# A Mamba block with an MLP and experts on one core: the order of products in the MLP's second bank, regrouped weights, four projections in another bank, and a later pin for the statistics

## Chip, core and metric

The kernel runs as one program on one core of a Trainium2 chip, in fp32. The metric is the device time of one execution in microseconds (us); lower is better. The engines are named as in the profile: PE is TensorE's matrix multiplication and PEld its loading of weights, DVE is VectorE, ACT is ScalarE, POOL is GpSimd, SP is SyncE, which here only starts DMAs. A line such as L422 is a line of the kernel before.

## What is computed

The input x has 2048 tokens (T) of 512 channels (D). Cut to what matters here:

```
u   = layernorm(x)
h   = u + mamba2(rmsnorm(u))            # in_proj 512->2576, causal conv of 4, scan in chunks of 128,
                                        # gated rmsnorm, out_proj 1024->512
x   = x + h + (silu(h2 @ gate) * (h2 @ up)) @ down       # h2 = rmsnorm(h), 512->2048->512
out = x + experts(layernorm(x))         # top 2 of 8 experts
```

## The kernel before

**Mamba.** The tokens are worked through in 8 blocks b of 256, each of two chunks of 128; t is the chunk, 0 to 15. While the chunks of block b are computed, `prepare(b + 1)` and `project(b + 1, ...)` make the next block's input.

`prepare` computes the layernorm statistics of its two chunks in `scales`: bn_stats and bn_aggr (L145, L146, VectorE), a square root (L190, ScalarE), a reciprocal (L191, VectorE). It normalizes to hn (L215, VectorE) and transposes hn on TensorE (L197); VectorE writes the transposed tile out of its bank with the norm weight (L201). The input projection is L333, its copy out of the bank L345 (ScalarE), the convolution L352 and L354 (VectorE) with L360 (ScalarE), and small halo copies L346, L347 (POOL).

`chunk` does one chunk's scan in pieces. POOL masks cum (L307). Two products are scaled by exponentials (L414, ScalarE, and L416, VectorE), VectorE makes xd (L422), and TensorE accumulates py (L432, L440) in bank y of pool `ps_y`, and the new state pst (L447) in bank tr. VectorE adds the skip term (yd, L453), adds to the state (L463) and multiplies by the gate (zs, L456). ScalarE squares zs (L476, L477), POOL sums the squares (L479), and TensorE adds over partitions (pms, L489, bank tr). L380 transposes the next chunk's x (ptx, bank tr). The projection po (L486) goes into bank y again. VectorE reads po at L497 to form h; POOL adds h to x (L498), ScalarE's queue stores that (L499), ScalarE squares h (L502), VectorE scales it (L505), and TensorE transposes h for the MLP (L197, bank tr; out by L201).

**MLP.** It works on 4 blocks fb of 512 tokens and 16 groups c of 128 hidden columns. The 512x512 tokens and channels, and the weights, are cut in halves and combined, so that one column group takes seven products of two matmuls each, 128x256, instead of eight. Four go to bank x1 (px) and three to bank x2 (py); each bank has one buffer while the MLP runs between Mamba pieces and two in the last block. In program order the px products are called first, t2, t3 and t4 here, the py products 2, 5 and 3:

- step 1: px first (copied by ScalarE, L760), then one py product, then a down projection pd (L699, added to the rows by VectorE, L700);
- step 2: px t2 (copied by ScalarE, L767), then one py product;
- step 3: px t3 (added to up by VectorE, L774), then one py product;
- step 4: px t4 (multiplied into a by VectorE, L779; POOL multiplies the other half, L780), then the other down projection.

Product 2 is added to a's first half by VectorE (L742) and goes through silu on ScalarE (L743). Product 5 is copied to up by ScalarE (L754). Product 3 adds onto product 5's result in the bank; VectorE adds it to a's second half (L748), and silu follows (L749). Product 3 so comes behind product 5 in any order, and it may write only when the copy L754 has read. Before, group 0 of each block takes 2, 5, 3, the others 5, 3, 2:

```
order = [p2, p5, p3] if c == 0 else [p5, p3, p2]
```

The weights of a group come in two tiles, early and late. In the first MLP block POOL forms sums and differences from the loaded weights (L530, L531, L541, L542) and stores both tiles to DRAM (L543, L544), from where the later blocks load them (L533, L546). The sums L530 and L531 of every group are pinned behind the squares' sums of chunk 1 (`summed_first`), which matters for the first groups.

**Order of the work.** A planner orders each engine's instructions by its own estimates. `tc.high_priority(AT_ONCE)` puts an instruction ahead of others; `tc.issue_after(x)` keeps instructions behind x on the same engine. TensorE alone follows the program's order from block 2 on. MLP blocks 0, 1 and 2 run between the Mamba pieces of blocks 2 to 7, two Mamba blocks for one MLP block, and the experts' routing between those; MLP block 3 runs alone from about 1080 us, and the experts come last. In `chunk`, `behind` and `newest_xd` remember the xd instructions (L422); `prepare` pins blocks 1 and 2 behind `behind`.

Of the kernel before, what the change touches and what calls it, by code (L numbers as in the profile page):

```python
# [8 lines left out]
F32 = mybir.dt.float32  # L9
I32 = mybir.dt.int32  # L10
AF = mybir.ActivationFunctionType
ALU = mybir.AluOpType
# [3 lines left out]
P = 128  # L16
T = 2048
D = 512
NK = D // P
# [5 lines left out]
NCH = TB // P  # L25
# [3 lines left out]
BPF = FB // TB  # L29
DFF = 2048  # L30
FH = FB // 2
FC = 128
NFC = DFF // FC
# [17 lines left out]
def mamba_mlp_moe(ctx, tc, x, w_in, w_out, w_gu, w_down, par, wr, wg, wu, wd, out):  # L51
# [3 lines left out]
    nc = tc.nc  # L55
# [9 lines left out]
    scratch = ctx.enter_context(tc.tile_pool(name="scratch", bufs=1, space=bass.MemoryType.DRAM))  # L65
# [26 lines left out]
    def load_w_in(pair):  # L92
# [15 lines left out]
        out=tri, in_=ones, pattern=[[1, P]], compare_op=ALU.is_ge, fill=0.0, base=0, channel_multiplier=-1  # L108
    )
    late = pw.tile([P, P], F32, name="late")  # L110
    nc.gpsimd.affine_select(
        out=late, in_=ones, pattern=[[-1, P]], compare_op=ALU.is_gt, fill=0.0, base=0, channel_multiplier=1
# [16 lines left out]
        out=upto, in_=ones[:, : NE * NE].rearrange("p (e f) -> p e f", e=NE), pattern=[[1, NE], [-1, NE]],  # L129
# [20 lines left out]
    early = const.tile([P, 1], F32, name="early")  # L150
# [18 lines left out]
    ps_y = psa_stack.enter_context(tc.tile_pool(name="ps_y", bufs=1, space=PSUM))  # L169
# [3 lines left out]
    def bank(kind, shape, name):  # L173
        pool, tag = use[kind]
        return pool.tile([P, *shape], F32, name=name, tag=tag)
# [10 lines left out]
    def scales(b):  # L186
        lo, hi = b * NCH, (b + 1) * NCH
        for t in range(lo, hi):
            stats(wa, res[t], mv[:, t, :])
        nc.scalar.activation(rboth[:, lo:hi], mv[:, lo:hi, 1], AF.Sqrt, bias=eps2, scale=1.0 + EPS)  # L190
        nc.vector.reciprocal(rboth[:, lo:hi], rboth[:, lo:hi])  # L191
# [11 lines left out]
    behind = None  # L203

    def prepare(b):
# [1 line left out]
        nonlocal behind  # L207
        hT = wa.tile([P, NK, TB], F32, name=f"hT{b}", tag="hT")
        hns = []
        with tc.issue_after(behind) if b in (1, 2) else ExitStack():  # L210
            scales(b)
            for j in range(NCH):
                t = b * NCH + j
                hns.append(wa.tile([P, D], F32, name=f"hn{t}", tag="tok", bufs=3))
                nc.vector.tensor_scalar(  # L215
                    hns[j], res[t], mv[:, t, 0:1], rboth[:, t : t + 1], ALU.subtract, ALU.mult
                )
        for j in range(NCH):
# [3 lines left out]
            if b == 0:  # L222
                behind = turned
# [19 lines left out]
        v, u, s, s2, acc = (small(n, 1) for n in ("v", "u", "s", "s2", "acc"))  # L243
# [142 lines left out]
    newest_xd = summed_first = None  # L386
    summed = None

    def chunk(b, j, dt, ncum, dtdec, cd, cum, ec, xb, cs, zs):

        nonlocal summed, summed_first, behind, newest_xd
        t = b * NCH + j
# [4 lines left out]
        y = zs[:, :, tok]  # L397

        for gp in range(2):
# [19 lines left out]
            if gp == 0 and t < NT - 1:  # L419
# [6 lines left out]
                behind, newest_xd = newest_xd or behind, added.ins  # L426
# [48 lines left out]
        with tc.high_priority(AT_ONCE):  # L475
            nc.scalar.activation(sq[:, 0:4, :], y[:, 0:4, :], AF.Square)  # L476
            nc.scalar.activation(sq[:, 4:8, :], y[:, 4:8, :], AF.Square)  # L477
            for n in (4, 2, 1):
                summed = nc.gpsimd.tensor_tensor(sq[:, 0:n, :], sq[:, 0:n, :], sq[:, n : 2 * n, :], ALU.add).ins  # L479
        if t == 1:  # L480
            summed_first = summed
        yield

        po = ps_y.tile([P, D], F32, name=f"po{t}", tag="y")
        for m in range(8):
            nc.tensor.matmul(po, y[:, m, :], w_o[:, m, :], start=(m == 0), stop=(m == 7))  # L486
        yield
# [28 lines left out]


    KH = NK // 2
    early_d = [scratch.tile([P, 3, KH, FC], F32, name=f"early{c}", tag=f"early{c}") for c in range(NFC)]
    late_d = [scratch.tile([P, 4, KH, FC], F32, name=f"late{c}", tag=f"late{c}") for c in range(NFC)]  # L520

    def load_early(fb, c):

        w = pmlp.tile([P, 4, KH, FC], F32, name="mg", tag="mg", bufs=3)
        if fb == 0:
            nc.sync.dma_start(out=w[:, 0], in_=w_gu[c, :, 0, 0])
            nc.sync.dma_start(out=w[:, 1], in_=w_gu[c, :, 1, 1])
            nc.sync.dma_start(out=w[:, 3], in_=w_gu[c, :, 1, 0])
            with tc.issue_after(summed_first):
                nc.gpsimd.tensor_tensor(w[:, 1], w[:, 3], w[:, 1], ALU.add)  # L530
                nc.gpsimd.tensor_tensor(w[:, 2], w[:, 1], w[:, 0], ALU.subtract)  # L531
        else:
            nc.sync.dma_start(out=w[:, 0:3], in_=early_d[c])  # L533
        return w

    def load_late(fb, c, w):

        v = pmlp.tile([P, 4, KH, FC], F32, name="ms", tag="mg", bufs=3)
        if fb == 0:
            nc.sync.dma_start(out=v[:, 2:4], in_=w_gu[c, :, :, 1])  # L540
            nc.gpsimd.tensor_tensor(v[:, 0], w[:, 0], w[:, 3], ALU.subtract)  # L541
            nc.gpsimd.tensor_tensor(v[:, 1], v[:, 2], w[:, 2], ALU.subtract)  # L542
            nc.gpsimd.dma_start(out=early_d[c], in_=w[:, 0:3])  # L543
            nc.gpsimd.dma_start(out=late_d[c], in_=v)  # L544
        else:
            nc.sync.dma_start(out=v, in_=late_d[c])  # L546
        return v

    def load_down(c):
# [152 lines left out]
    def feed_forward(fb):  # L702

        nonlocal mlp_w, newest
        if fb == 0:
            w = load_early(0, 0)
            mlp_w = w, load_late(0, 0, w)
        b11, b21, b22, t1, t2, t3, t4 = sums(fb)
        rows = []
        pair = None  # L710
        made = {}

        def product(ps, w, m, first=True):
            for k in range(KH):
                nc.tensor.matmul(  # L715
                    ps, w[:, k], m[:, k], start=(first and k == 0), stop=(k == KH - 1), skip_group_check=True
                )

        early, late = mlp_w
        for c in range(NFC):
            more = fb < NFB - 1 or c < NFC - 1
            to = (fb, c + 1) if c < NFC - 1 else (fb + 1, 0)
            if more:
                coming = load_early(*to)
            if c == 1:
                for j in range(NJ):
                    rows.append(wk.tile([P, D], F32, name=f"r{fb}_{j}", tag="row", bufs=5))  # L730
                    nc.sync.dma_start(out=rows[j], in_=resd[fb * NJ + j])
            if c > 1 and c % 2 == 0:
                pair = [made.pop(n) for n in (c - 2, c - 1)]
            a = wk.tile([P, 2, FH], F32, name=f"a{fb}_{c}", tag="a", bufs=4)
            up = wk.tile([P, FH], F32, name=f"up{fb}_{c}", tag="up", bufs=2)
            x1 = bank("g", [FH], f"px{fb}_{c}")
            x2 = bank("u", [FH], f"py{fb}_{c}")

            def p2():
                product(x2, late[:, 2], b21)  # L740
                with tc.high_priority(AT_ONCE):
                    nc.vector.tensor_tensor(a[:, 0], a[:, 0], x2, ALU.add)  # L742
                nc.scalar.activation(a[:, 0], a[:, 0], AF.Silu)  # L743

            def p3():
                product(x2, late[:, 1], b22, False)
                with tc.high_priority(AT_ONCE):
                    nc.vector.tensor_tensor(a[:, 1], a[:, 1], x2, ALU.add)  # L748
                nc.scalar.activation(a[:, 1], a[:, 1], AF.Silu)  # L749

            def p5():
                product(x2, early[:, 1], t1)
                with tc.high_priority(AT_ONCE):
                    nc.scalar.copy(up, x2)  # L754


            order = [p2, p5, p3] if c == 0 else [p5, p3, p2]
            product(x1, early[:, 0], b11)
            with tc.high_priority(AT_ONCE):
                nc.scalar.copy(a[:, 0], x1)  # L760
            order[0]()
            if pair:
                mlp_down(fb, rows, 2 * (c % 2), pair)
            yield
            product(x1, early[:, 2], t2, False)
            with tc.high_priority(AT_ONCE):
                nc.scalar.copy(a[:, 1], x1)  # L767
            order[1]()
            if more:
                coming = coming, load_late(*to, coming)  # L770
            yield
            product(x1, late[:, 0], t3, False)
            with tc.high_priority(AT_ONCE):
                nc.vector.tensor_tensor(up, up, x1, ALU.add)  # L774
            order[2]()
            yield
            product(x1, late[:, 3], t4, False)
            with tc.high_priority(AT_ONCE):
                nc.vector.tensor_tensor(a[:, 0], a[:, 0], x1, ALU.mult)  # L779
            nc.gpsimd.tensor_tensor(a[:, 1], a[:, 1], up, ALU.mult)  # L780
            if pair:
                mlp_down(fb, rows, 2 * (c % 2) + 1, pair)
            newest = a.rearrange("p h q -> p (h q)")
            made[c] = newest, load_down(c)
            if more:
                early, late = coming
            yield
        if more:
            mlp_w = coming
        pair = [made.pop(n) for n in (NFC - 2, NFC - 1)]  # L790
        for j in range(NJ):
            mlp_down(fb, rows, j, pair)
        yield
        yield from route(fb, rows)

    coming = prepare(0)
    for _ in range(3):
        hT = next(coming)  # L800
# [393 lines left out]
```

## Time and profile before

| | |
|---|---|
| three runs | 1588.06, 1590.36, 1590.94 us |
| median | 1590.36 us |
| profiled execution: its own time | 1588.24 us |
| its span | 1586.2 us |
| mean granted clock of TensorE | 0.991 |

The profile is of one execution. Its span runs from its first to its last instruction; 2.0 us of its time lie around that. Busy time counts an engine's own instructions. A timeline's row has start, duration, engine, line, operation, output <- inputs, shapes and count; brackets at its end give the idle time of the engine just before and what ended it, where that is known ("issue" is a wait for nothing that the profile shows). A row with several instructions prints the time from the first's start to the last's end. A list of waits has the total idle time, the times and the longest. Windows give each engine's busy time in a stretch, the instructions in brackets, and the granted clock, where 1.00 is full speed.

### The profile page before, as it was taken

What the parts mean: (1) busy time and instruction counts of PE and PEld (TensorE: products, weight loads), DVE (VectorE), ACT (ScalarE), POOL (GpSimd) and SP (SyncE); (2) the same over time, 40 slices, a digit from 0 to 9 for tenths busy, and PEclk for the clock granted to TensorE, in tenths of its full rate; (3) what the DMA queues carried; (4) which work ended last, traced back from release to release, by engine and by line L of the source; (5) the groups of instructions that cost most, each with busy time, mean ns of one, the idle gap of its engine ahead of it and who ended that gap; (6) DMA issues with size and microseconds to landing.
All of it is one profiled execution on the core that took longest, in us unless ns stands there. A gap on an engine that the chain in (4) does not pass through costs nothing. (4 is left out here: it accounts for less than half of the span.)

```text
span 1586.2 us, 19139 instructions
## 1 busy us (share of the span) xinstructions
PE 1543.2 (97%) x6308; PEld 1052.1 (66%) x6308; DVE 776.1 (49%) x2018; ACT 726.8 (46%) x1325; POOL 427.1 (27%) x542
## 2 busy tenths in 40 slices
PE   9999999999999999999999999999999999999996
PEld 7556576667676776766676667666777666655553
DVE  7586765645647365546555454434454352222221
ACT  6786866836683775456546533222211221111110
POOL 3543335434342212121212212011111123333331
PEclk9899999999999999999999999999999999999999
DMA  9444434644544454343354432229777233333332
GB/s 313 123 127 155 131 124 165 207 145 155 163 166 166 159 181 129 112 135 120 107 171 143 166 107 87 90 90 298 241 239 237 83 61 61 66 63 64 67 67 34
DMA packets 126432, 218.68 MB, mean 138 GB/s; under 512 B 11584, under 2 KB 71488, under 8 KB 126336
## 3 DMA queue, kind: packets, MB, share of 16 engines
q1 hardware_dynamic: 105088, 166.08, 33.1%
q0 software_dynamic: 12320, 35.13, 9.8%
q10 hardware_dynamic: 8928, 16.26, 2.8%
q8 instruction: 52, 0.85, 0.2%
q14 instruction: 44, 0.36, 0.1%
HBM read 176.01 MB, written 41.42 MB: 137 GB/s over the span
## 5 line engine op out<-in xcount | busy, mean ns | idle before, releaser
L699 PE MATMUL pd<-md,a 128*128 128x512 f32 x512 | 239.2, 594 | 0.0
L333 PE MATMUL pm<-hT,wi 128*128 128x256 f32 x768 | 182.7, 384 | 0.8 <-ACT pre L345 0.8
L700 DVE TENSOR_TENSOR r<-r,pd 128x512 f32<-128x512 f32 x128 | 87.4, 684 | 148.6 <-PE pd L699 147.8
L333 PEld LDWEIGHTS pm<-hT,wi 128*128 128x128 f32 x768 | 141.0, 190 | 25.1 <-issue 6.1
L699 PEld LDWEIGHTS pd<-md,a 128*128 128x128 f32 x512 | 97.5, 191 | 75.2 <-issue 66.6
L354 DVE SCALAR_TENSOR_TENSOR ca<-pre,params,ca 128x256 f32<-128x256 f32 x288 | 140.4, 541 | 0.3
L780 POOL TENSOR_TENSOR a<-a,up 128x256 f32<-128x256 f32 x64 | 47.9, 748 | 315.9 <-DVE up L774 256.7
L715 PE MATMUL py<-h2T,ms 128*128 128x256 f32 x512 | 132.0, 380 | 0.9 <-ACT up L754 0.7
L333 PE MATMUL pz<-hT,wi 128*128 128x256 f32 x512 | 122.5, 393 | 1.1 <-DMA wi<-in_w_in 1.1
L1050 PE MATMUL epg<-ew,xgT 128*128 x312 | 118.1, 460 | 0.4 <-issue 0.2
L1050 PE MATMUL epu<-ew,xgT 128*128 x312 | 117.8, 459 | 0.0
L486 PE MATMUL po<-w_o,zs 128*128 128x512 f32 x256 | 113.3, 593 | 1.1 <-DVE yd L453 0.8
L333 PEld LDWEIGHTS pz<-hT,wi 128*128 128x128 f32 x512 | 98.5, 198 | 18.2 <-issue 3.7
L1071 PE MATMUL epd<-ew,ehT 128*128 (+1 forms) x234 | 107.1, 593 | 1.0 <-DVE ehT L1064 1.0
L715 PEld LDWEIGHTS py<-h2T,ms 128*128 128x128 f32 x512 | 95.0, 190 | 17.7 <-DVE a L748 1.9
L414 ACT ACT_TABLE_LOAD x66 | 84.7, 1283 | 34.6 <-DVE ncum L281 33.0
L414 ACT ACTIVATE cum<-cum,ncum 128x128 f32<-128x128 f32 x256 | 85.6, 393 | 13.3 <-POOL cum L307 11.7
L486 PEld LDWEIGHTS po<-w_o,zs 128*128 128x128 f32 x256 | 48.1, 190 | 57.5 <-issue 53.3
L1031 POOL DMA_INDIRECT xg<-xnd,idx x39 | 38.7, 991 | 175.6 <-PE pt L197 173.6
L1050 PEld LDWEIGHTS epu<-ew,xgT 128*128 128x128 f32 x312 | 59.3, 190 | 33.0
L1077 POOL DMA_INDIRECT out<-ey,idx x39 | 62.0, 1590 | 67.0 <-DVE ey L1076 40.8
L199 ACT COPY xgT<-pt 128x512 f32<-128x512 f32 x39 | 22.8, 586 | 117.7 <-PE pt L197 117.7
(250 smaller groups left out, 2577.9 us busy)
## 6 DMA issues: line engine op xcount, KB each, us to landing
wi<-in_w_in SPq DMA_DIRECT2D x80, 512.0 KB, 3.8
ms<-late SPq DMA_DIRECT2D x48, 512.0 KB, 3.8
mg<-early SPq DMA_DIRECT2D x48, 384.0 KB, 3.1
md<-in_w_down SPq DMA_DIRECT2D x64, 256.0 KB, 3.9
cum<-rowsd SPq DMA_DIRECT2D x32, 512.0 KB, 4.5
late<-ms POOLq DMA_DIRECT2D x16, 512.0 KB, 4.3
ec<-rowsd SPq DMA_DIRECT2D x60, 128.0 KB, 4.0
xnd<-xn ACTq DMA_DIRECT2D x28, 256.0 KB, 4.0
```

Of the source, the lines that this page charges most:

```text
L333: nc.tensor.matmul(pm[:, m, :], w[:, k, m * P : (m + 1) * P], hT[:, k, :], start=(k == 0), stop=(k == NK - 1))
L354: nc.vector.scalar_tensor_tensor(ca, pre[:, m, k : k + TB], cw[:, k : k + 1], ca, ALU.mult, ALU.add)
L414: nc.scalar.activation(lt[:, half, i], lt[:, half, i], AF.Exp, bias=ncum[:, j, h : h + 1])
L486: nc.tensor.matmul(po, y[:, m, :], w_o[:, m, :], start=(m == 0), stop=(m == 7))
L699: nc.tensor.matmul(pd, a[:, j * P : (j + 1) * P], d, start=(m == 0), stop=(m == 1))
L700: nc.vector.tensor_tensor(rows[j], rows[j], pd, ALU.add)
L715: nc.tensor.matmul(ps, w[:, k], m[:, k], start=(first and k == 0), stop=(k == KH - 1), skip_group_check=True)
L780: nc.gpsimd.tensor_tensor(a[:, 1], a[:, 1], up, ALU.mult)
L1031: nc.gpsimd.indirect_dma_start(out=xg, out_offset=None, in_=src, in_offset=bass.IndirectOffsetOnAxis(ap=idx[:, n : n + 1], axis=0))
L1050: nc.tensor.matmul(ps, xT[:, k, :], w[:, lo : lo + EI], start=(k == 0), stop=(k == NK - 1))
L1071: nc.tensor.matmul(pd, hT[:n, m, :], w[:n, NG + m * D : NG + (m + 1) * D], start=(m == 0), stop=(m == len(ET) - 1))
L1077: nc.gpsimd.indirect_dma_start(out=out, out_offset=bass.IndirectOffsetOnAxis(ap=idx[:, n : n + 1], axis=0), in_=y, in_offset=None, compute ...
```

## The change

In the second bank all groups take products 2, 5, 3. So the weights for product 2 are needed in step 1, for product 5 in step 2 and for product 3 in step 3, and the tiles are regrouped: early has four parts, late three. The host lays out the gate and up weights so that a group's four parts, gate top, gate bottom, up top, up bottom, are contiguous and arrive in the first MLP block by one DMA of 512 KB where there were three of 128 KB; what late loads is one part instead of two. In later blocks early is 512 KB instead of 384 and late 384 instead of 512.

The pin of the POOL sums on the weights is the squares' sums of chunk 0 instead of chunk 1. In the order of instructions on POOL six operations on the weights of groups 0 and 1, with three DMA issues, then stand between chunk 0's squares' sums and chunk 0's residual add L498; one mask of chunk 2 (L307) stands between the second and the third issue.

The projections po of chunks 0 to 3 are written to bank x1, which the MLP does not use until chunk 4. The statistics and hn of blocks 3 to 7, not pinned before, stand behind the newest xd.

```
-        with tc.issue_after(behind) if b in (1, 2) else ExitStack():
+        with tc.issue_after(behind if b < 3 else newest_xd) if b else ExitStack():
...
-        if t == 1:
+        if t == 0:
             summed_first = summed
...
-        po = ps_y.tile([P, D], F32, name=f"po{t}", tag="y")
+        po = ps_y.tile([P, D], F32, name=f"po{t}", tag="y") if t >= BPF * NCH else bank("g", [D], f"po{t}")
...
-    early_d = [scratch.tile([P, 3, KH, FC], F32, name=f"early{c}", tag=f"early{c}") for c in range(NFC)]
-    late_d = [scratch.tile([P, 4, KH, FC], F32, name=f"late{c}", tag=f"late{c}") for c in range(NFC)]
+    early_d = [scratch.tile([P, 4, KH, FC], F32, name=f"early{c}", tag=f"early{c}") for c in range(NFC)]
+    late_d = [scratch.tile([P, 3, KH, FC], F32, name=f"late{c}", tag=f"late{c}") for c in range(NFC)]
...
         if fb == 0:
-            nc.sync.dma_start(out=w[:, 0], in_=w_gu[c, :, 0, 0])
-            nc.sync.dma_start(out=w[:, 1], in_=w_gu[c, :, 1, 1])
-            nc.sync.dma_start(out=w[:, 3], in_=w_gu[c, :, 1, 0])
+            nc.sync.dma_start(out=w, in_=w_gu[c])
             with tc.issue_after(summed_first):
-                nc.gpsimd.tensor_tensor(w[:, 1], w[:, 3], w[:, 1], ALU.add)
-                nc.gpsimd.tensor_tensor(w[:, 2], w[:, 1], w[:, 0], ALU.subtract)
+                nc.gpsimd.tensor_tensor(w[:, 3], w[:, 2], w[:, 3], ALU.add)
+                nc.gpsimd.tensor_tensor(w[:, 2], w[:, 3], w[:, 0], ALU.subtract)
         else:
-            nc.sync.dma_start(out=w[:, 0:3], in_=early_d[c])
+            nc.sync.dma_start(out=w, in_=early_d[c])
...
-            nc.sync.dma_start(out=v[:, 2:4], in_=w_gu[c, :, :, 1])
-            nc.gpsimd.tensor_tensor(v[:, 0], w[:, 0], w[:, 3], ALU.subtract)
-            nc.gpsimd.tensor_tensor(v[:, 1], v[:, 2], w[:, 2], ALU.subtract)
-            nc.gpsimd.dma_start(out=early_d[c], in_=w[:, 0:3])
-            nc.gpsimd.dma_start(out=late_d[c], in_=v)
+            nc.sync.dma_start(out=v[:, 2], in_=w_gu[c, :, 3])
+            nc.gpsimd.tensor_tensor(v[:, 0], v[:, 2], w[:, 2], ALU.subtract)
+            nc.gpsimd.tensor_tensor(v[:, 1], w[:, 1], w[:, 2], ALU.subtract)
+            nc.gpsimd.dma_start(out=early_d[c], in_=w)
+            nc.gpsimd.dma_start(out=late_d[c], in_=v[:, 0:3])
...
-                product(x2, late[:, 2], b21)
+                product(x2, early[:, 1], b21)
...
-                product(x2, early[:, 1], t1)
+                product(x2, early[:, 3], t1)
...
-            order = [p2, p5, p3] if c == 0 else [p5, p3, p2]
...
-            order[0]()
+            p2()
...
-            order[1]()
+            p5()
...
-            order[2]()
+            p3()
...
-            product(x1, late[:, 3], t4, False)
+            product(x1, late[:, 2], t4, False)
```

On the host, `w_gu` gets one more `.reshape(NFC, P, 4, NK // 2, FC)`.

More of the change, by code (lines that the diff above doesn't have):

```diff
@@ L539, in load_late @@
         if fb == 0:
-            nc.sync.dma_start(out=v[:, 2:4], in_=w_gu[c, :, :, 1])
-            nc.gpsimd.tensor_tensor(v[:, 0], w[:, 0], w[:, 3], ALU.subtract)
-            nc.gpsimd.tensor_tensor(v[:, 1], v[:, 2], w[:, 2], ALU.subtract)
-            nc.gpsimd.dma_start(out=early_d[c], in_=w[:, 0:3])
-            nc.gpsimd.dma_start(out=late_d[c], in_=v)
+            nc.sync.dma_start(out=v[:, 2], in_=w_gu[c, :, 3])
[3 more added lines that the diff above has]
+            nc.gpsimd.dma_start(out=late_d[c], in_=v[:, 0:3])
         else:
-            nc.sync.dma_start(out=v, in_=late_d[c])
+            nc.sync.dma_start(out=v[:, 0:3], in_=late_d[c])
         return v
@@ L1168 @@
     )
-    w_gu = np.stack([a["gate_w"], a["up_w"]]).reshape(2, 2, NK // 2, P, NFC, FC).transpose(4, 3, 0, 1, 2, 5)
+    w_gu = np.stack([a["gate_w"], a["up_w"]]).reshape(2, 2, NK // 2, P, NFC, FC).transpose(4, 3, 0, 1, 2, 5).reshape(NFC, P, 4, NK // 2, FC)
     ins = {
```

## Prediction

> **What bounds the kernel now.** I read the busy times of the engines first, then TensorE's waits, then the timeline around each wait.
>
> ```profile
> PE 1543.2 (97%) x6308; PEld 1052.1 (66%) x6308; DVE 776.1 (49%) x2018; ACT 726.8 (46%) x1325; POOL 427.1 (27%) x542
> ...
> L715 PE MATMUL py<-h2T,ms 128*128 128x256 f32 x512 | 132.0, 380 | 0.9 <-ACT up L754 0.7
> ```
>
> TensorE is busy for 97% of 1586.2 us, and the change takes no product away. Only its remaining waits and its half-clock stretches can be won. Summing what each of its instructions starts later than the usual step of its kind gives some 60 us, 30 of them before 205 us. The last column of the L715 row (idle before, and who ended it) holds the one wait of today that the new order can multiply; it returns under the rivals.
>
> ```profile
> PE px L715 <- DVE a L779: 7.9, 7, 2.4
> PE py L432 <- issue: 6.6, 2, 3.4
> ```
>
> These are TensorE's two largest entries (total, times, longest). The first is the next column group's product waiting until VectorE has multiplied the last one out of its bank. The second shows no releaser; the timeline does:
>
> ```profile
> 198.67 0.74 DVE L497 SCALAR_TENSOR_TENSOR h<-po,ry,h 128x512 f32<-128x512 f32 x1
> ...
> 199.52 1.54 PE L432 MATMUL py<-ec,sdiag 128*128 128x128 f32 x8 [3.20 <-issue]
> ...
> 201.79 1.22 DVE L422 TENSOR_TENSOR xd<-xbt,dtdec 128x1024 f32<-128x1024 f32 x1
> ...
> 203.62 1.00 DVE L215 TENSOR_SCALAR hn<-x,mv,rboth 128x512 f32<-128x512 f32 x2
> ...
> 207.00 0.66 PE L197 MATMUL pt<-ident,hn 128*128 128x128 f32 x4 [0.78 <-DVE h2T L201]
> ```
>
> L432 writes the bank that the chunk's projection (po) holds until L497 has read it: TensorE starts 0.11 us after that read ends. Chunk 1 has the same picture (L497 from 119.52, L432 at 120.36).
>
> The waits cost clock as well. The columns are TensorE, weight loads, VectorE, ScalarE, GpSimd, granted clock, DMA share and GB/s:
>
> ```profile
> 196.40:199.70 3.30, 0.18 (x1) 0.21 (x2) 3.27 (x9) 3.24 (x7) 0.20 (x1) 1.00 0.00 0
> 199.80:203.10 3.30, 3.30 (x14) 2.85 (x13) 3.30 (x13) 2.63 (x6) 1.14 (x1) 0.54 0.20 79
> ...
> 715.20:718.50 3.30, 0.93 (x7) 0.71 (x7) 3.30 (x11) 3.24 (x5) 0.00 (x0) 1.00 0.00 0
> 718.60:722.00 3.40, 3.40 (x9) 2.39 (x9) 2.70 (x10) 2.05 (x6) 0.19 (x1) 0.55 0.00 0
> ```
>
> After a window in which TensorE mostly stood, about 3.4 us run at a clock of 0.54: half of the work of 3.4 us is lost, 1.7 us. A wait that brings such a window is so worth its length plus 1.7.
>
> **Part by part.** I worked from the order of instructions on each engine in both kernels, with durations from the trace before.
>
> **A, chunk 1's projection in the MLP bank (100 to 128 us).** Gone: the wait at 116.2 (3.6), its half clock (1.65), and, as the projection no longer needs the y bank, its wait on L453 (0.67); the wait of the input projection on ScalarE's copy at 100.76 (0.98) changes with ScalarE's order. Together 6.9. What is late next: TensorE arrives earlier than its inputs. The transposes of x wait for the state sum L463, which ends at 107.17 where TensorE now comes at about 105.8 (1.4); the second half of the projection waits for L456 (0.6); the sum of squares L489 waits for GpSimd's adds, done at 113.31 (1.65); the transpose of h 0.5. Together 4.15. **Net -2.8.** Below: -6.9 if these inputs also come earlier; above: 0.
>
> **B, chunk 3's projection and the statistics of block 3 (183 to 211 us).** Gone: waits of 3.27 (L432), 0.44 (L453) and 0.95 (transpose of h), and the half clock, 1.56: 6.2. New by the same reasoning: transposes of x 1.05, sum of squares 1.8 (GpSimd ends at 194.18), transpose of h 0.85: 3.7. The pin moves every instruction of the statistics behind xd L422: the two bn_stats, the aggregate, the root on ScalarE with its table load, the reciprocal and hn. VectorE's order then is xd, bn_stats twice, aggregate, h2T L201, two sums for the MLP, reciprocal, hn L215. Nothing is queued behind hn that TensorE needs sooner, but TensorE's next item is the transpose of hn. Without any earlier arrival: h2T ends at 206.94, plus 0.68 and 0.68 (L689, L690), 0.15 and 0.50 gives 208.95, against 206.22 when TensorE was ready for it: 2.7. The bn_stats and aggregate ahead add 1.55 (4.3), TensorE's earlier arrival 0.85 (5.1), the root with its table load 1.57 (6.7). I take 5.1, because VectorE has no idle row between 183 and 204 us with which to come earlier. Such a wait brings one half-clock window, 1.7. Sum: -6.2 + 3.7 + 5.1 + 1.7 = **+4.3**. Ends: 6.7 and two windows, +7.6; hn not late at all, -2.5.
>
> **C, the six GpSimd operations on the first weights, behind chunk 0's squares instead of chunk 1's.** They take 0.78 each (two of L530 last 1.58) and move, with three DMA issues, into the idle of GpSimd from 75.3 us, ahead of a select of 1.09 and of chunk 0's residual add L498. 75.3 + 4.7 + 1.1 + 1.9 for the issues gives 83.0 instead of 81.30. ScalarE's DMA issue and its Square stand behind that add, so h is some 1.6 late; its transpose had 0.95 to spare (h ends at 87.68, transpose at 88.67). **+0.7**; ends 0 (cover of the product run at 84.1) and +2.
>
> The row of 201.79 has xd alone: 1.22. At 260.38 below, with L498 of GpSimd beside it, the same operation takes 2.52. The Trainium skill ("SBUF — State Buffer", "Who interferes with whom") speaks against C with a reason for this: a VectorE instruction with two SBUF inputs contends with a GpSimd instruction that reads SBUF. No wait of TensorE at 75 to 83 us hangs on such a pair in the trace; by the rule alone one xd more would pay 1.3, inside the +2.
>
> **D, the products' order (205 to 1080 us).** Its best case first:
>
> ```profile
> 260.38 2.52 DVE L422 TENSOR_TENSOR xd<-xbt,dtdec 128x1024 f32<-128x1024 f32 x1 [0.22 <-ACT sq L502]
> ...
> 264.50 0.69 DVE L700 TENSOR_TENSOR r<-r,pd 128x512 f32<-128x512 f32 x1 [0.59 <-PE pd L699]
> 265.10 0.41 DVE L779 TENSOR_TENSOR a<-a,px 128x256 f32<-128x256 f32 x1
> 265.57 1.13 PE L715 MATMUL px<-h2T,mg 128*128 128x256 f32 x4 [1.11 <-DVE a L779]
> ```
>
> L779 had to wait for silu (264.43 to 264.85), because product 2 came last; so the row add L700 stood ahead of it. With 2 first, silu is done a step sooner and L779 comes before L700, behind xd alone. This saves the 1.27 (excess over the usual step) here and at 411.4: -2.5. At 332.0 and 479.8 other work stands ahead of it: 0. At 715.1 L779 was late by 2.53 through a bn_stats that waited for its DMA, L700 and convolutions; this and the half clock shown above go: -4.2. Waits of the third product on L748 in the third MLP block (0.31 + 0.15 + 0.15) go: -0.6. New: product 3 adds onto product 5's bank and must wait for ScalarE's copy L754. In the third MLP block, steps 2 and 3 stand back to back, with 0.3 us to spare; two groups have a table load or Square between, +1.1. **Sum -6.2.** Ends: -7.3 without the new waits, +3.5 under the slow rival.
>
> The Trainium skill ("TensorE: Matmul & The Clock Gate", "What's actually happening") has the clock drop after at least one idle window of about 3.4 us. The row at 715.20 has TensorE busy for 0.93 of 3.30, its longest gap 2.4, and the clock fell all the same. By the rule read as a gap's length, 715.1 would be worth 2.5 instead of 4.2.
>
> At nothing: early weights grow from 384 to 512 KB (3.1 to 3.8 us, beside a column group of some 9.5 us until they are needed), late ones shrink as much; without that cover 0.7 a group. SP's queue loses 32 issues. The last MLP block (from 1080) has two buffers a bank and its copies wait for nothing: 0.
>
> **Sum:** -2.8 + 4.3 + 0.7 - 6.2 = -4.0. The profiled execution took 1588.24 (span 1586.2), so 1584.2; it lies 2.1 below the median 1590.36, against which I forecast **1586.4**.
>
> **The rivals.** *No effect (same):* B at +7.6 and C at +2 leave -2.8 + 7.6 + 2 - 6.2 = +0.6: 1591.0. For it: VectorE's full queue at 183 to 204. Against: the half clock needs a window met badly twice.
>
> *Slower:* the copy L754 is late in the third MLP block. Before, one group in this order shows the price:
>
> ```profile
> 1088.18 0.35 ACT L754 COPY up<-py 128x256 f32<-128x256 f32 x1
> ...
> 1088.59 1.13 PE L715 MATMUL py<-h2T,ms 128*128 128x256 f32 x4 [0.72 <-ACT up L754]
> ```
>
> A silu with its table load (1086.57) stood ahead of the copy. With 0.72 in 15 groups, D is -7.3 + 10.8 = +3.5, the sum +5.7: 1596.1. It ends over 0.2% slower from about 0.55 a group on. For it: ScalarE's queue there holds table loads of 1.28. Against: the orders show something between the two copies in two groups only.
>
> *Much faster:* the statistics are not late, B is -2.5: the sum is -10.8, 1579.6. Against: VectorE's rows in B.
>
> That the regrouping does nothing at all is excluded by the orders; that A and B merely hand the wait on is the case of no effect.
>
> **Numbers.** A difference under 0.2% (3.2 us) cannot be told from none by measurement here. Forecast 0.38, much faster 0.14, no effect 0.20, slower 0.28. Of the forecast's case 0.02 falls within 0.2%: faster 0.50, same 0.22, slower 0.28. The range takes in the fast rival and the slow one, 1579.5 to 1596.5.
>
> **What would show it.** A and B: L432 of chunks 1 and 3 starts without a wait, and waits stand before L489; the first transpose of hn of block 3 waits about 5 us. C: L498 of chunk 0 starts near 83. D: "px <- DVE a L779" falls from 7.9 to about 3, no half clock at 718, "py <- ACT up L754" grows from 0.7 to some 2. I am wrong if the transpose of hn waits under 2 or over 8 us, or if L754 ends waits in most groups.

## The result and the profile after

| | before | changed |
|---|---|---|
| runs | 19 | 19 |
| median | 1589.85 us | 1588.53 us |
| lowest to highest | 1585.72 to 1592.45 | 1584.36 to 1593.92 |
| profiled span | 1586.2 | 1585.9 |

The ratio is 0.9996, with a 95% interval of 0.9986 to 1.0005: no difference that can be measured. The forecast was 4.0 us faster.

The page and TensorE's list of waits (total, times, longest) of the changed kernel:

```profile
PE 1539.6 (97%) x6308; PEld 1050.8 (66%) x6308; DVE 778.7 (49%) x2018; ACT 732.0 (46%) x1329; POOL 420.7 (27%) x542
```

```profile
PE pt L197 <- DVE hn L215: 8.3, 2, 8.0
PE pc L269 <- DVE dA L266: 4.4, 1, 4.4
PE pms L490 <- POOL sq L479: 3.0, 2, 1.8
PE px L714 <- DVE a L776: 2.5, 4, 0.7
...
PE pt L197 <- DVE h L506: 1.6, 2, 1.4
...
PE py L714 <- ACT up L753: 1.3, 2, 0.7
```

Both large waits of before are smaller or gone: "px <- DVE a" fell from 7.9 to 2.5, and L432 is not in the list. In their place stands one wait of 8.0 us for hn.

To see where the time went, I compared the start of the same TensorE instruction in both traces (changed minus before, in us):

| time in the trace before | changed minus before | what lies in the stretch that ends there |
|---|---|---|
| 96.7 | -0.2 | first block; GpSimd's moved operations |
| 146.3 | -3.3 | chunk 1 (A) |
| 178.7 | -4.2 | chunk 2 |
| 235.7 | +1.7 | chunk 3, statistics of block 3 (B) |
| 530.5 | -1.9 | MLP block 0 and part of 1 |
| 602.5 | +0.3 | MLP block 1 |
| 723.5 | -3.8 | MLP block 1; the place at 715 |
| 906.6 | -0.5 | MLP block 2 |
| 1082.4 and all later ones | -0.3 | end of MLP block 2; MLP block 3 and experts alike |

So 5.8 us are lost in 57 us around chunk 3. The timeline there, in the changed kernel:

```profile
199.31 1.22 DVE L422 TENSOR_TENSOR xd<-xbt,dtdec 128x1024 f32<-128x1024 f32 x1
...
200.44 1.28 DVE L145 BATCH_NORM_STATS2 bn<-x 128x6 f32<-128x512 f32 x2
...
204.40 0.30 ACT L190 ACTIVATE rboth<-mv,singles 128x2 f32<-128x2 f32 x1
...
204.93 1.98 DVE L215 TENSOR_SCALAR hn<-x,mv,rboth 128x512 f32<-128x512 f32 x2
...
206.61 1.09 PE L197 MATMUL pt<-ident,hn 128*128 128x128 f32 x4 [8.00 <-DVE hn L215]
```

Everything that the pin put behind xd comes in a row: bn_stats, the root, and hn 5.6 us after xd began. TensorE had transposed h at 198 and stood until then. The windows show its clock at half from 201.5 us on, while it still stands and for about 4 us of its work behind that:

```profile
201.50:204.80 3.30, 0.00 (x0) 0.00 (x0) 2.37 (x7) 3.26 (x6) 2.07 (x2) 0.50 0.09 31
204.90:208.20 3.30, 1.59 (x6) 1.53 (x7) 2.97 (x5) 3.27 (x8) 1.28 (x2) 0.50 0.02 5
208.30:211.60 3.30, 3.30 (x11) 2.64 (x10) 0.58 (x2) 1.06 (x1) 0.00 (x0) 0.60 0.00 0
```

### The profile page after: what moved, and what is told of

Its sections match the earlier page's. It is cut to its first block, busy times and chain, and to the rows that moved or that the text cites. A ratio compares the mean times of both kernels' runs of the same rounds, so it can differ in the third digit from the quotient of the medians.

```text
span 1585.9 us, 19000 instructions
## 1 busy us (share of the span) xinstructions
PE 1539.6 (97%) x6308; PEld 1050.8 (66%) x6308; DVE 778.7 (49%) x2018; ACT 732.0 (46%) x1329; POOL 420.7 (27%) x542
## 5 line engine op out<-in xcount | busy, mean ns | idle before, releaser
L354 DVE SCALAR_TENSOR_TENSOR ca<-pre,params,ca 128x256 f32<-128x256 f32 x288 | 143.7, 547 | 0.6
L333 PE MATMUL pz<-hT,wi 128*128 128x256 f32 x512 | 118.6, 385 | 0.0
L414 ACT ACTIVATE cum<-cum,ncum 128x128 f32<-128x128 f32 x256 | 86.2, 393 | 15.9 <-POOL cum L307 13.8
L771 DVE TENSOR_TENSOR up<-up,px 128x256 f32<-128x256 f32 x64 | 26.8, 419 | 105.8 <-PE px L714 93.4
L1068 PEld LDWEIGHTS epd<-ew,ehT 128*128 128x128 f32 (+1 forms) x234 | 44.1, 190 | 46.0 <-issue 37.3
```

The source lines that it names most:

```text
L333: nc.tensor.matmul(pm[:, m, :], w[:, k, m * P : (m + 1) * P], hT[:, k, :], start=(k == 0), stop=(k == NK - 1))
L354: nc.vector.scalar_tensor_tensor(ca, pre[:, m, k : k + TB], cw[:, k : k + 1], ca, ALU.mult, ALU.add)
L414: nc.scalar.activation(lt[:, half, i], lt[:, half, i], AF.Exp, bias=ncum[:, j, h : h + 1])
L1068: nc.tensor.matmul(pd, hT[:n, m, :], w[:n, NG + m * D : NG + (m + 1) * D], start=(m == 0), stop=(m == len(ET) - 1))
```

## The experiments

A difference is the ratio to the kernel before, run again beside each experiment, less 1, times 1589.85; the 95% interval stands in brackets. Where a trace is compared, it is by the start of the same TensorE instruction, as above. The theory at the start was that the pin on block 3's statistics gives back what the rest wins; its rival, that TensorE only waits for the next input at the same places.

### Without the later pin

```
-        with tc.issue_after(behind if b < 3 else newest_xd) if b else ExitStack():
+        with tc.issue_after(behind) if b in (1, 2) else ExitStack():
```

> The changed kernel without its pin on the statistics of blocks 3 to 7 (only blocks 1 and 2 pinned, as before). Theory (the pin in block 3 gives back what the other parts win): VectorE's order becomes xd, reciprocal, h2T, hn; hn is ready some 3 us earlier against its transpose, so the wait of 8.0 us at the first transpose of hn falls to about 3.3 and the half clock behind it goes; 5 us less than the changed kernel, about 1583.5. Rival (any order leaves hn late, the wait is only handed on to another input of TensorE at the same place): no less than 1 us off, 1587.5 to 1588.5.

Measured: 1583.06 us, -6.8 [-9.2, -4.5]: 6.2 less than the changed kernel. Its timeline at the same place:

```profile
201.51 1.22 DVE L422 TENSOR_TENSOR xd<-xbt,dtdec 128x1024 f32<-128x1024 f32 x1
202.65 0.16 DVE L191 RECIPROCAL rboth<-rboth 128x2 f32<-128x2 f32 x1
202.72 0.67 DVE L201 TENSOR_TENSOR h2T<-pt,params 128x512 f32<-128x512 f32 x1
203.31 1.95 DVE L215 TENSOR_SCALAR hn<-x,mv,rboth 128x512 f32<-128x512 f32 x2
...
204.00 1.09 PE L197 MATMUL pt<-ident,hn 128*128 128x128 f32 x4 [2.93 <-DVE hn L215]
```

hn comes 1.8 us after xd began instead of 5.6, and the wait is 2.9 instead of 8.0. The rival falls: 5.1 us of the wait are the pin's. The other 2.9 stay without it.

### The pin on blocks 4 to 7 only

```
+        with tc.issue_after(behind if b < 3 else newest_xd) if b not in (0, 3) else ExitStack():
```

> The changed kernel with the pin on blocks 4 to 7 but not on block 3. If the pin of blocks 4 to 7 is worth nothing by itself: equal to the kernel with no later pin, about 1583.5. If it is what removed the wait at 715 us (by keeping a bn_stats that waits for its DMA off the head of VectorE's queue): 3 to 4 us less than the kernel with no later pin. Rival (wait handed on): 1587.5 or more.

Measured: 1583.64, -6.0 [-8.4, -3.5], as without any later pin. The pin of the later blocks does nothing that can be measured on top of the other parts. The wait at 715 us is gone without it too: there the first experiment's trace gains 4.3, as the changed kernel's does.

The transpose of hn waits 2.9 here as in the first experiment. There the clock was at half behind it (0.64 from 202.4 to 205.7 us), here it stays full (1.00 from 201.7 to 205.0). So the same wait can bring the half clock or not, and a wait's length alone does not tell.

### The pin alone

The changed kernel's line (the one with the minus in the first experiment), put into the kernel before.

> The kernel before with the later pin of the statistics alone. Theory (the pin costs by itself, because hn comes behind xd, two bn_stats, an aggregate, the root and two sums): hn of block 3 some 4 us later than in the kernel before, less 1.7 that h of chunk 3 comes earlier without the statistics in front of it: 2 to 5 us slower, 1592 to 1595. Rival (the pin costs only where the projection no longer waits for its bank, since otherwise TensorE stands at that place anyway): within 1 us of before, 1589 to 1591.

Measured: 1594.89, +3.3 [+1.1, +5.4]. Its trace waits 5.4 for hn and still 3.6 for L432 at chunk 3, and loses 7.1 us there. The pin costs by itself, bank or no bank; the rival falls. At 715 us this trace gains 3.3: with the bn_stats pinned elsewhere, px waits 0.8 for L779 there instead of 2.4, and no half clock follows. So the pin and the order of products each remove that wait alone, and together they remove it once.

### The products and the weights alone

The kernel before with the changed products, weights and tiles, without the other three parts.

> The kernel before with the order of products and the regrouped weights alone; projections, statistics and the GpSimd pin as before. Theory (read from the two traces: 6 us won at four places, 4 given back by the copies L753 and the half clock in MLP blocks 1 and 2): 2 us less than before, about 1587.9. Rival (the sum of the prediction): 6.2 less, about 1583.7. If the pin had done the work at 715 us: 2 us more than before.

Measured: 1585.93, -4.5 [-6.5, -2.2]. The trace's sum from 236 to 1082 us is -4.0. In it the place at 715 is worth 4.3, as it is in the changed kernel, though nothing is pinned later here: the products and their weights, which this run does not separate, remove that wait. The theory's -2 was too little; the prediction's -6.2 lies inside the interval but 2.2 above the trace's sum.

### The bank alone

```
-        po = ps_y.tile([P, D], F32, name=f"po{t}", tag="y")
+        po = ps_y.tile([P, D], F32, name=f"po{t}", tag="y") if t >= BPF * NCH else bank("g", [D], f"po{t}")
```

> The kernel before with the projections of chunks 0 to 3 in bank x1 alone. Theory: chunk 1 -3 as in the changed kernel's trace; chunk 3 loses the wait on the y bank and its half clock (-5.3), takes the new waits on the state sum and the squares' sum (+3.7) and an hn wait of about 3: +1 to -2; the sum -2 to -5, 1585 to 1588. Rival (waits handed on in full): 1589 to 1590.

Measured: 1590.01, -1.7 [-4.8, +1.1]: undecided by the times. By its trace the stretch of chunk 1 gains 1.0 and that of chunk 3 loses 0.9. L432 no longer waits, and in its place stand the sum of squares (1.9 at the longest), the transpose of h (2.6) and the transpose of hn (2.9). At chunk 1 the half clock is not gone either; it follows the wait for h (0.50 from 128.1 to 131.3 us). That is the rival, as far as one trace can show it: the wait is handed on.

### The GpSimd pin alone

```
-        if t == 1:
+        if t == 0:
             summed_first = summed
```

> The kernel before with the GpSimd operations on the first weights behind chunk 0's squares instead of chunk 1's, nothing else. Theory (nothing waits for them at either place): 0, 1589 to 1591. Rival (the prediction's step C): +0.7, with an upper end of +2; the other rival, that GpSimd free at 115 to 120 us lets the residual add of chunk 1 come earlier: -1.

Measured: 1585.07, -5.4 [-7.6, -3.2]. Theory and both rivals miss; this part, which was to cost 0.7, wins about as much as the products. The trace's stretch from 96.7 to 146.3 us gains 3.5 of it. The other 1.9 this trace does not show: its execution took 1587.43, 2.4 above the median, and had lost 1.7 ahead of 96.7 us. Before, at chunk 1:

```profile
114.88 1.58 POOL L530 TENSOR_TENSOR mg<-mg 128x256 f32<-128x256 f32 x2
...
116.53 2.20 DVE L354 SCALAR_TENSOR_TENSOR ca<-pre,params,ca 128x256 f32<-128x256 f32 x3
116.62 1.83 POOL L531 TENSOR_TENSOR mg<-mg 128x256 f32<-128x256 f32 x2
...
119.52 0.74 DVE L497 SCALAR_TENSOR_TENSOR h<-po,ry,h 128x512 f32<-128x512 f32 x1
```

and with the GpSimd pin moved:

```profile
117.31 1.27 DVE L354 SCALAR_TENSOR_TENSOR ca<-pre,params,ca 128x256 f32<-128x256 f32 x3
...
118.95 0.74 DVE L497 SCALAR_TENSOR_TENSOR h<-po,ry,h 128x512 f32<-128x512 f32 x1
...
119.80 1.13 PE L432 MATMUL py<-ec,sdiag 128*128 128x128 f32 x8 [1.21 <-issue]
```

The three convolutions take 1.27 instead of 2.20 when no GpSimd operation lies beside them. With their neighbours L352 and L354, VectorE needs 2.85 us from the first of them (116.10) to L497, where it needed 5.09 before (from 114.43). That is the 2.2 by which L432's wait shrinks. L497 frees the bank earlier, L432 waits 1.2 instead of 3.4, and the half clock does not follow. So the moved pin and the new bank remove the same wait.

### What of the GpSimd operations costs: reads or the queue

Two kernels with the GpSimd pin moved put something useless where the operations had been. In the kernel before, five operations on the weights stand there (L530 and L531 twice, L542). The first adds six additions of a tile of zeros:

```
+        if t == 1:
+            with tc.issue_after(summed):
+                for n in range(6):
+                    nc.gpsimd.tensor_tensor(zero[:, 0:256], zero[:, 0:256], zero[:, 256:512], ALU.add)
```

> The kernel before with the GpSimd pin moved to chunk 0, and six additions 128x256 of a tile of zeros on GpSimd, which no one needs, at the place that the weight operations left (behind chunk 1's squares). Theory (what the moved operations cost before is the convolutions L354 beside them: VectorE and GpSimd both read two tiles of SBUF): L354 is drawn out again, L432 of chunk 1 waits about 3.6 us again, the half clock returns: 3 to 5 us slower than with the moved pin alone, 1588 to 1590. Rival (what cost was the weights' DMA issues or their place in GpSimd's queue, not reads beside VectorE): as with the moved pin alone, 1585.

The second has `nc.gpsimd.memset(zero, 0.0)` nine times instead.

> As the run with the six additions, but with nine memsets 128x512 of the same tile instead (0.52 us each in the trace of before, 4.7 in all): GpSimd is as busy at the same place and reads nothing. Theory (reads contend): as with the moved pin alone, 1585, the wait at L432 of chunk 1 about 1.4. Rival (GpSimd's queue being busy is what costs): 1588 to 1590, as the additions.

Measured: 1590.74, +1.3 [-0.3, +3.0], with the additions; 1589.07, -1.1 [-2.7, +0.3], with the memsets. Additions, then memsets:

```profile
118.40 2.21 DVE L354 SCALAR_TENSOR_TENSOR ca<-pre,params,ca 128x256 f32<-128x256 f32 x3
```

```profile
119.44 1.26 DVE L354 SCALAR_TENSOR_TENSOR ca<-pre,params,ca 128x256 f32<-128x256 f32 x3
...
119.89 4.59 POOL L485 MEMSET zero<- 128x512 f32 x8
...
124.45 2.09 POOL L502 TENSOR_TENSOR x<-x,h 128x512 f32<-128x512 f32 x1
...
129.45 0.63 PE L197 MATMUL pt<-ident,h 128*128 128x128 f32 x4 [2.95 <-DVE h L509]
```

Reads draw L354 out, 2.21 against 1.26; writes do not. L432 waits 2.5 with the additions and 1.4 with the memsets, against 3.4 before and 1.2 with the moved pin alone. The half clock, which the theory expected with the additions, does not come (1.00 from 122.8 to 126.1 us). The times of L354 agree with the Trainium skill ("SBUF — State Buffer", "Who interferes with whom"): a VectorE instruction with two SBUF inputs contends with a GpSimd instruction that reads SBUF, not with one that only writes it.

L354 is not all of it. With the memsets the convolutions' first step, L352, took 1.82 where it takes 0.35 alone:

```profile
117.70 1.82 DVE L352 TENSOR_SCALAR ca<-pre,params 128x256 f32<-128x256 f32 x1
...
118.84 0.53 POOL L485 MEMSET zero<- 128x512 f32 x1
```

A GpSimd operation of the scan (L403, 117.46 to 118.91) and the first memset lie beside it, and it ends 0.15 after the memset. Which of the two held it was not tested.

And the rival is right as well. The residual add (here L502) stands behind the memsets until 124.45, the store of x behind it on ScalarE's queue, then h, and TensorE waits 2.95 for h. Both ways cost; in the stretch from 96.7 to 146.3 the two kernels gain 2.3 and 1.6, where the moved pin alone gains 3.5. That explains 1.2 and 1.9 of the 6.7 and 4.3 us by which they are slower.

In their traces another 2.9 and 3.4 lie ahead of 96.7 us, where the same instructions stand in the same order as with the moved pin alone. There the weights' operations cost at their new place. With the additions:

```profile
79.60 1.10 POOL L307 TENSOR_SCALAR_AFFINE_SELECT cum<-cum 128x1024 f32<-128x1024 f32 x1
...
80.74 0.40 ACT L414 ACTIVATE cum<-cum,ncum 128x128 f32<-128x128 f32 x1 [3.03 <-POOL cum L307]
...
82.77 0.41 PE L287 MATMUL psum<-dA,late 128*128 128x32 f32 x2 [1.73 <-ACT ry L140]
```

The mask L307 stands behind the moved operations and starts at 79.60 instead of 76.66. ScalarE waits 3.03 for it and makes ry (L140) later; TensorE waits 1.73 for that, and its clock is at half behind (0.50 from 86.2 to 89.5). From 75.4 to 88.7 us TensorE loses 5.1, with the memsets just as much. The trace of the moved pin alone loses nothing there: TensorE had already waited 4.6 for dA at 68 us, while GpSimd ran ahead (see the last section). How often executions take one way or the other, the times do not tell.

### The products and the GpSimd pin, without bank and later pin

> The changed kernel without the later pin and with all projections in bank y again: the order of products, the weights and the GpSimd pin are left. Theory (the bank wins nothing once GpSimd's operations no longer stand beside the convolutions at 115 us, and costs about 1 us at chunk 3): as fast as the kernel without the later pin or 1 faster, 1581.5 to 1583; the sum of the two parts measured alone (4.4 and 5.4) gives 1580. Rival (the bank has a gain of its own, 2.8 at chunk 1): 1585.5 or more.

Measured: 1581.46, -8.0 [-10.0, -5.7]. The two parts alone add up to -9.9. The rival falls, and no gain of the bank is to be seen: with it (first experiment) it is -6.8, an interval that overlaps.

### Product 5 ahead of px t2

Without the later pin, and in step 2:

```
+            p5()
             product(x1, early[:, 2], t2, False)
             with tc.high_priority(AT_ONCE):
                 nc.scalar.copy(a[:, 1], x1)
-            p5()
```

> The changed kernel without the later pin, and in step 2 of each column group product 5 goes ahead of px t2, so that ScalarE's copy of product 5 has one product (0.86 us) more before px t3 and product 3 need it. Theory (what part D gives back in MLP blocks 1 and 2 are waits behind that copy): the waits "py <- ACT up" and "px <- DVE up", together 1.4 to 2.5 us in the traces with the new order, go; 1.5 less than without the later pin, about 1581.5. Rival (a copy that is late comes from ScalarE's whole queue, so px t2's copy is late instead): no difference, 1583.

Measured: 1604.22, ratio 1.0087 [1.0067, 1.0108], 21 us more than without the later pin. One row of its waits says why:

```profile
PE px L714 <- ACT a L765: 16.2, 31, 1.5
```

Px t3 adds onto t2's bank and must wait for the copy of t2 (L765 here). Product 5 between them had been its cover, 0.86 us a time. Now it is gone in 31 groups, 0.5 on average. Most of the loss comes after 906 us, where steps 2 and 3 stand back to back. The waits behind the copy of product 5 fell as expected, to one of 0.5, but they were the smaller ones: the cure costs more than the complaint. The rival named the right copy, that of t2, but not the reason or the size: it had expected no difference.

### hn of block 3 at once

Without the later pin, and statistics and hn of block 3 given priority:

```
-        with tc.issue_after(behind) if b in (1, 2) else ExitStack():
+        with tc.issue_after(behind) if b in (1, 2) else tc.high_priority(AT_ONCE if b == 3 else 0):
```

> The changed kernel without the later pin, and the statistics and hn of block 3 given priority, so that VectorE does them ahead of chunk 3's h, xd and h2T. Theory (hn is late by VectorE's order alone): the 3 us that hn's transpose still waits for without the pin go, 1 to 3 us less than without the later pin, 1580 to 1582. Rival (VectorE is full there, and what goes ahead pushes h of chunk 3 and xd back by as much): no difference, 1583, with a longer wait at the transpose of h or at the state.

Measured: 1580.30, ratio 0.9948 [0.9928, 0.9967], -8.3, the lowest median of all. It is 2.8 less than without the later pin by the medians, as the theory had it, but the two intervals overlap. Chunk 3's stretch now gains 2.2 where it lost 5.8 in the changed kernel. What hn's transpose waits for is no longer hn but its bank:

```profile
198.19 0.63 PE L197 MATMUL pt<-ident,h 128*128 128x128 f32 x4 [1.28 <-DVE h L506]
...
200.28 0.66 PE L197 MATMUL pt<-ident,hn 128*128 128x128 f32 x4 [1.46 <-DVE h2T L201]
```

The same with all projections in bank y:

> As the kernel with hn of block 3 at once (1580.3), but with all projections in bank y. Theory (the bank at chunk 3 pays only when hn is not what TensorE waits for next; then it saves the half clock at 200 us and part of the wait): about 2 slower, 1582 to 1583. Rival (the bank is worth nothing in any company): 1580.

Measured: 1582.20, ratio 0.9954 [0.9940, 0.9967]. The medians are 1.9 apart as expected, but the intervals overlap. The traces differ more: at chunk 3 this kernel loses 1.7 where the other gains 2.2. That the bank pays only with hn early is likely, not shown by the times.

## Why the prediction was off, point by point

The measured -0.6 us (ratio 0.9996) is inside the range and is the size of the rival "no effect" (+0.6), which had a chance of 0.20. The forecast of -4.0 did not come. By the stretches of the trace the parts came to -0.2 (up to 96.7 us, C's new place; +0.7 foreseen), -3.1 (A; -2.8), -0.8 (chunk 2; nothing), +5.8 (B; +4.3) and -2.0 (D; -6.2). So the step that failed most is D's term for the new waits, and after it B's wait for hn. That A's stretch comes out near its number is luck, since another part of the change gained it.

- **A, chunk 1's projection in the other bank (-2.8).** The stretch gained 3.1, but not by the bank. The step that failed is the bank's net gain: alone it removes the wait at 116.2, meets the new waits, keeps the half clock at a later place and gains 1.0. The moved GpSimd pin alone gains 3.5 there, and both together no more. That TensorE then waits for the state, the squares' sum and h is confirmed (0.6, 1.8 and 1.4).
- **C, the GpSimd operations (+0.7).** Wrong in sign. I priced what the six operations push away where they arrive, and found nothing to count where they leave. The row for it was there: L354 three times in 2.20 beside L530 and L531. I applied the rule on shared reads to the place of arrival only. What I priced there was TensorE's wait for h of chunk 0; it did not appear, and the changed kernel is level with before at 96.7 us. But that is the way of this execution, which had waited 4.4 for dA just before. The traces with the additions and the memsets lose 5.1 at the place of arrival, through the mask L307 that I had counted as time on GpSimd without asking who waits for it.
- **B, the statistics of block 3 (+4.3).** Right in mechanism and sign, short in size: the trace has +5.8. The mis-sized term is the wait for hn, put at 5.1 with 6.7 as its end; it was 8.0. I let TensorE arrive 0.85 us earlier; it arrived 3.5 earlier by before's clock (4.2 us ahead at 178.7, transposing h at 198.0 against 205.6), because the waits that I counted as new came to 1.7 instead of 3.7. What TensorE did not wait for there it waited for at hn. The 8.0 lie at the prediction's own sign of being wrong ("over 8 us"). The half clock came as foreseen.
- **D, the products (-6.2).** The terms at 260 and 411 us (1.27 each) and at 715 (4.2) came as worked out: 1.4, 1.4 and 4.3. Two more places gained 0.4 each that I had at nothing. What failed is the price of the new waits, 1.1. Between 236 and 1082 us the trace of the changed kernel gains 7.9 and loses 5.9, that of the products alone gains 9.3 and loses 5.3. From 530 to 602 us 2.2 were lost in the changed kernel and 2.3 with the products alone, most of it at one wait that I had not listed: px t4 behind the addition L771, which stood behind a convolution that waited for ScalarE's copy. In MLP block 2, counted from 0, the wait for L753 showed as forecast:

```profile
860.35 0.35 ACT L753 COPY up<-py 128x256 f32<-128x256 f32 x1
...
860.76 1.13 PE L714 MATMUL py<-h2T,ms 128*128 128x256 f32 x4 [0.60 <-ACT up L753]
```

  In that block the profiled execution also lost a half-clock stretch of 1.7 us (868.8 to 872.2, clock 0.63) that the trace of the products alone does not have.
- **The slow rival.** Its mechanism is real (two waits for L753, the longest 0.7) but met two groups, not 15, as the orders had said. The other transfers cost nothing: no wait of TensorE for the weights is listed.

In sum, two gains of about 4 to 5 us each (C and D) stand against one loss (the pin: 3.3 put in alone, 6.2 won by taking it out); no gain of the bank shows beside them. Medians of 1580.3 to 1583.1 us were had with the loss left out.

## What to carry to other kernels

Two edits that remove the same wait are worth it once: ask of each wait what ends it, and what ends that. When an operation moves, price the place that it leaves as carefully as the place it goes to: its neighbours were perhaps slower for it, and whatever it is put ahead of has readers of its own. Before putting an instruction behind another, ask which engine's next instruction is its reader, above all when the same change lets that engine arrive earlier; and before swapping two products, ask whose copy the one between them was covering.

## What the runs showed that I had not expected

The first 100 us hold a lottery. Up to chunk 1's projection the kernels before and with the bank alone have the same instructions in the same order on each engine. Yet at about 84 us the traces of all kernels lie from 4.3 us ahead of before (products alone) to 3.6 behind (memsets). In before, the additions and the memsets, the clock is at half from 46 to 56 us. In all the others it stays full there and TensorE is 4 to 6.5 us ahead at 64 us. Then, in all of these but one, VectorE's small chain L257 meets GpSimd: changed kernel, then products alone, which missed it:

```profile
60.64 3.40 DVE L257 SCALAR_TENSOR_TENSOR acc<-acc,s 128x32 f32<-128x32 f32 x3
...
60.92 1.03 POOL L462 TENSOR_TENSOR state<-state,cd 128x512 f32<-128x512 f32 x1
```

```profile
60.76 0.93 DVE L257 SCALAR_TENSOR_TENSOR acc<-acc,s 128x32 f32<-128x32 f32 x3
...
62.27 1.04 POOL L462 TENSOR_TENSOR state<-state,cd 128x512 f32<-128x512 f32 x1
```

Three instructions of 0.2 us took 3.4, and TensorE waited 4.4 for dA. An early start thus bought a collision. Differences of a few us between two single traces are therefore read by stretch, from a point behind this one. Why some executions take the one way and some the other was not tried.
